# First stage of a four-layer convolution and attention network: the input norm moved a unit ahead on all engines, and the first query projection moved ahead of the value statistics

## The chip, the core and the metric

The kernel runs on one NeuronCore of a Trainium2 chip, as one program with one launch. The metric is the device time of one execution in microseconds (us). Lower is better. All arithmetic is float32.

## The reference, cut to what matters

The network has four residual layers on an image batch `x` of 8 images, 384 channels, 32x32 pixels. Only the head of layer 0 matters here:

```python
def _dwproj(x, dw, g, b, pw):                 # once each for q, k and v
    y = conv2d(x, dw, pad=1, groups=C)        # 3x3, one filter per channel
    y = gelu(batchnorm(y, g, b))              # mean and variance over all 8 images
    return einsum('oc,bchw->bohw', pw, y)     # 384 x 384 projection

h = groupnorm(x, 32 groups)                   # per image and group of 12 channels
q, k, v = _dwproj(h, ..q), _dwproj(h, ..k), _dwproj(h, ..v)
out = softmax(q^T k * hd**-0.5) v             # 8 heads of 48 channels, 1024 pixels
x = x + batchnorm(w_out @ out)
# layers 1 to 3: mixture of experts, depthwise + pointwise convolution,
# deformable attention; each on groupnorm(x), each added to x
```

The batch norm of q, k and v needs the statistics of the convolved images of the whole batch. So the convolutions of all eight images come first, their raw results go to DRAM, and only then can the first gelu, projection and attention start. That first part is called the first stage below.

## The kernel before, in words

**Units and items.** The stage works on 16 tiles `xs` of 128 partitions x 3072 numbers. Two tiles (`j` = 0, 1) make one *unit* `u`, and there are eight units. A unit is convolved in *items*, listed in `work` (lines 397 to 400): `y0 a1 y1 a2 v0` for units 0 to 5, `y0 a1 y1 a2` for unit 6, and `y0 a1 y1 a2 v-1 v0` for unit 7, which makes 40 items numbered `n`. Each item is a row of small matmuls on quarters and eighths of the array (line 554), into four PSUM banks: items of odd `n` take four single banks, items of even `n` two double ones. So the matmuls of an item can start when the item two before it has been copied out. ScalarE (ACT) copies the banks to a tile `y` (line 565; the pool of `y` has four buffers), VectorE (DVE) takes `bn_stats` of the four rows (line 571), and SyncE (SP) writes the tile to DRAM in four transfers (line 585).

**The norm.** Before a unit is convolved, its tiles are normalised in place. `norm(u)` (lines 326 to 394) gives five steps: `begin(0)` and `begin(1)` take statistics of the two tiles on DVE (lines 338, 341); `finish` is a chain of ten small DVE operations with one power on GpSimd (POOL) (lines 353 to 372), which ends in the scales `gss`; `apply(0)` and `apply(1)` each scale half of both tiles with two ACT instructions (line 384), after each of which POOL clears two border rows (line 387).

**Who sets the order.** The whole stage stands under a manual schedule: each engine executes its instructions in the order in which this loop issues them. In the item loop (from line 501) the steps of `norm(u + 1)` are issued during unit `u`, ahead of the item's matmuls, by the table

```python
        AT = {0: 0, 1: 1, 2: 2, 3: 3, 4: 3}
```

which says: `begin(0)` ahead of the unit's item 0, `begin(1)` ahead of item 1, `finish` ahead of item 2, and both `apply` steps, four ACT instructions in a row, ahead of item 3 (`a2`). Loads of later tiles and of the first raw images `g` are issued two per item on SP, in order with the `y` writes.

**The end of the stage.** Ahead of the last item but one, `spread_qk` (line 405) turns the statistics of q and k into scales: its scratch tile `room` is taken from the pool of `y`, so it waits until the write of an older `y` is done. After that item ACT applies gelu to the raw q image and the raw k image of image 0 (line 594), and DVE takes the moments of `x` (24 short `bn_aggr`, line 144). After the last item `spread_v` (line 459) does the same for v: statistics, a matmul `pmovev`, a chain on DVE, and the scales of v.

**The start of the attention.** Outside the manual schedule, only ACT keeps its issue order; the other engines' orders come from a scheduler. gelu of the v image, then `project(0, 0, v, h)` for q and k in two halves each (line 705), copied out in turn by ACT and DVE (`evac`), then `values` (line 678), scores (line 791), exponentials (line 798), and the weighted sum `pav` (line 806). The value tiles `vt` are zeroed by POOL (lines 653 and 660), with a dependency on the scales of v. Raw images live in the pool `im` of five buffers (`image`), taken in turn.

Of the kernel before, what the change touches and what calls it, by code (L numbers as in the profile page):

```python
# [7 lines left out]
F32 = mybir.dt.float32  # L8
# [5 lines left out]
N = H * W  # L14
P = 128
# [40 lines left out]
def tile_kernel(ctx: ExitStack, tc: tile.TileContext, i: dict, out: bass.AP):  # L56
# [196 lines left out]
    w0p = w0_ctx.enter_context(tc.tile_pool(name="w0", bufs=1))  # L253
    w_in = [w0p.tile([P, KC, C], F32, name=f"{nm}_sb") for nm in ("wq0", "wk0", "wv0")]

    with ExitStack() as pa:
        wa = pa.enter_context(tc.tile_pool(name="a_w", bufs=1))
        xa = pa.enter_context(tc.tile_pool(name="a_x", bufs=6))
# [63 lines left out]
        zv = wa.tile([P, 8, 2], F32, name="zv")  # L322
        fqk = wa.tile([P, 2, 2, KC], F32, name="fqk")
        fv = wa.tile([P, 2, KC], F32, name="fv")

        def norm(u):

            k, h = divmod(u, 2)
            mv = mvs[u % 2]
            turned = sa.tile([P, 2, 32], F32, tag="gp_t", name=f"gt{u}")  # L330
            rows = sa.tile([P, 2, 2, 16], F32, tag="gp_r", name=f"gr{u}")
            ss = sa.tile([P, 2, 32], F32, tag="gp_ss", name=f"gss{u}")
            small_ = sa.tile([P, 40], F32, tag="gp_s", name=f"gs{u}")

            def begin(j):
                for g in range(2):
                    for c in range(KC):
                        nc.vector.bn_stats(
                            xst[:, 2 * h + g, 2 * k + j, c, :], xs_of[2 * u + j][:, g * KC + c, :]
                        )  # L340
                    nc.vector.bn_aggr(
                        mv[:, :, 2 * j + g],
                        xst[:, 2 * h + g, 2 * k + j].rearrange("p c s -> p (c s)"),
                    )

            def finish():

                def owned(t):
                    return t.rearrange("p (g m d) -> p g m d", g=2, d=4)[:, :, :, 1:3]

                m8, v8, rs = small_[:, 0:2], small_[:, 2:4], small_[:, 4:6]
                dm, var, wide = small_[:, 8:40], turned[:, 1, :], [P, 2, 16]
# [19 lines left out]
                nc.vector.transpose(  # L372
                    ss.rearrange("p t y -> p (t y)"), rows.rearrange("p t g y -> p (t g y)")
                )

            def apply(g):
                for j in range(2):
                    n = 2 * j + g
                    d = xs_of[2 * u + j][:, g * KC : g * KC + KC, :]
                    sc, sh = ss[:, 0, n : n + 1], ss[:, 1, n : n + 1]  # L380
                    if u == 0 and j == 1:
                        nc.vector.tensor_scalar(d, d, sc, sh, ALU.mult, ALU.add)
                    else:
                        nc.scalar.activation(d, d, AF.Identity, bias=sh, scale=sc)
                    for e, row in enumerate((0, HALF - W)):
                        f = d[:, :, row : row + W]
                        nc.gpsimd.tensor_tensor(  # L387
                            f, f, mrow[:, e : e + 1].unsqueeze(2).to_broadcast([P, KC, W]),
                            ALU.mult,
                        )  # L390
# [12 lines left out]
        steps = {}  # L403

        def spread_qk():

            room = ya.tile([P, 4, HALF], F32, tag="y", name="room")
            zs, nv, ng = (zy, zqk.rearrange("p c g s -> p (c g) s")), (3, 2), 16
            both = [
                room[:, 0, 256 * t : 256 * t + 2 * n * ng].rearrange(  # L410
                    "p (v s g) -> p v s g", v=n, s=2
                ) for t, n in enumerate(nv)
            ]
            v0 = 0
            for z, n, dst in zip(zs, nv, both):
# [1 line left out]
                v0 += n  # L417
            yield
            pm = bank("pmove")
            for t, n in enumerate(nv):  # L420
                nc.tensor.matmul(
                    pm[:, 256 * t : 256 * t + 2 * n * ng], lhsT=sels[:, t, :],
                    rhs=room[:, 0, 256 * t : 256 * t + 2 * n * ng], start=True, stop=True,
                )
# [5 lines left out]
            fy = room[:, 3, :6].rearrange("p (v s) -> p v s", v=3)  # L430
            nc.vector.reduce_sum(fy.rearrange("p v s -> p (v s)"), got, AX.X)
            got = room[:, 2, :64].rearrange("p (x g) -> p x g", g=8)
            nc.vector.tensor_tensor(
                got, pm[:, 256:320].rearrange("p (x g) -> p x g", g=8),
                msk[:, 16:24].unsqueeze(1).to_broadcast([P, 8, 8]), ALU.mult,
            )
            f = room[:, 3, 8:16]
# [21 lines left out]
        def spread_v():  # L459

            both = sa.tile([P, 32], F32, tag="bothv", name="bothv")
            masked(zv, 2, 5, both.rearrange("p (c s g) -> p c s g", c=2, s=2))
            pm = bank("pmovev")
            nc.tensor.matmul(pm[:, :32], lhsT=sels[:, 1, :], rhs=both, start=True, stop=True)
            got = sa.tile([P, 4, 8], F32, tag="gotv", name="gotv")
# [30 lines left out]
        for f in norm(0):  # L496
            f()
        quads = [slice(32 * r, 32 * r + 32) for r in range(4)]
        loads = []
        LOADS = {0: (8, 9, 10), 1: (11, 12), 3: (13,), 4: (14, 15)}  # L500
        for n, (u, kind, s) in enumerate(work):
            k, h = divmod(u, 2)
            at = n - first[u]
            if at == 0:
# [99 lines left out]
    ost = const.tile([P, KC, 2 * B, 6], F32, name="ost")  # L604
# [35 lines left out]
    with ExitStack() as pb:  # L640
# [53 lines left out]
            load_image(fetched[b, t], o_dram[b] if t else x_img[b])  # L694

        def project(b, pr, v, h):
            if h == 0:
                qks[b, pr, v] = qp.tile([P, N], F32, tag=f"qk{v}", name=f"qk{v}_{b}_{pr}")
# [4 lines left out]
            pq = bank(f"pq{v}_{b}_{pr}_{h}")  # L703
            for c in range(KC):
                nc.tensor.matmul(  # L705
                    pq,
                    lhsT=w_in[v][:, c, pr * P : (pr + 1) * P],
                    rhs=rows_of(acts[b][v][:, c, :], h * H // 2, (h + 1) * H // 2) if v == 0
                    else acts[b][v][:, c, h * HALF : (h + 1) * HALF],
                    start=(c == 0),  # L710
                    stop=(c == KC - 1),
                )
# [1431 lines left out]
```

## Time and profile before

| | |
|---|---|
| median of 3 runs | 3521.9 us (3520.86 to 3522.46) |
| the profiled execution's own time | 3521.31 us |
| its span, first to last instruction | 3519.5 us, so 1.8 us lie around it |
| mean granted TensorE clock over the span | 0.981 |
| line 554, all matmuls of the stage | 3840 x, 175.7 us busy in sum, 66.1 us idle ahead of them |
| first matmul of the stage | 24.44 us |
| end of the stage's last item on TensorE | 243.42 + 1.25 = 244.67 us |
| first score matmul of image 0 | 267.03 us |
| first weighted sum `pav` of image 0 | 272.80 us |

The profile is one execution. A row of its timeline gives start, duration, engine, source line, operation, tiles, and in brackets how long the engine was idle before it and what ended that. PE is TensorE's matmuls, DVE VectorE, ACT ScalarE, POOL GpSimd, SP the queue that issues transfers. In the answer by stretches each row gives the busy time of each engine, then the granted TensorE clock, the mean busy share of the 16 DMA engines and the GB/s moved.

### The profile page before, as it was taken

Reading aid. Unit: us, or ns where it says so; the run is one execution under the profiler, and the core shown is the slowest. Engines: PE = TensorE matmul, PEld = TensorE weight load, DVE = VectorE, ACT = ScalarE, POOL = GpSimd, SP = SyncE. Lnnn points to the kernel's source line nnn. Section 1 sums busy time; section 2 is a strip of 40 time slices with the busy share of each in tenths; the row PEclk is TensorE's granted clock in tenths of the full one; section 3 lists DMA queues with packets and bytes.
Section 4 is the critical chain, followed back from the end, with each engine's and each line's share of the span. In section 5 each row is a group of like instructions: output and inputs, shape, how many; then the busy total and the mean of one; then the engine's idle time right before and its main releaser. Section 6 shows DMA issues by size and latency. Waiting matters only on the chain.

```text
span 3519.5 us, 44915 instructions
## 1 busy us (share of the span) xinstructions
PE 3379.2 (96%) x18599; PEld 1468.1 (42%) x18599; DVE 1695.2 (48%) x2881; ACT 1298.0 (37%) x1514; POOL 211.3 (6%) x231
## 2 busy tenths in 40 slices
PE   5879999999999999998999999999999999999897
PEld 2433434343434343433344444444443444534434
DVE  7762232323232323234266475564755647556663
ACT  4554444444444444433212323223233232332222
POOL 2110000000000000000000100101001010010112
PEclk9889999999999999999999999999999999999898
DMA  9872212112121212021700110101101011110000
GB/s 350 264 212 70 57 54 52 55 49 60 45 66 39 73 33 80 25 80 63 282 21 21 35 57 28 43 21 35 57 35 39 18 35 57 35 39 18 0 31 25
DMA packets 86259, 234.01 MB, mean 66 GB/s; under 512 B 21672, under 2 KB 21896, under 8 KB 79130
## 3 DMA queue, kind: packets, MB, share of 16 engines
q1 hardware_dynamic: 83882, 222.75, 20.0%
q10 hardware_dynamic: 1248, 4.72, 0.3%
q8 instruction: 150, 2.46, 0.3%
q0 software_dynamic: 912, 3.53, 0.3%
q14 instruction: 67, 0.55, 0.1%
HBM read 145.77 MB, written 75.59 MB: 63 GB/s over the span
## 4 chain that ended last, share of the span: by engine, by line
PE 41%; DVE 9%; DMA 1%; ACT 1%; POOL 0%; issue 0%; DVEq 0%; ACTq 0%; POOLq 0%; SPq 0%
PE y L1473 12%; PE ph L1452 9%; DVE y L1548 5%; PE pq L1593 4%; PE pw L1556 3%; PE pf L1900 3%; PE s L1771 2%; PE pav L1797 2%; DVE hd L1438 1%; DMA o<-o 1%; PE pk L1746 1%; PE pv L1755 1%; PE xsb L1732 1%; PE pss L1810 1%; PE plog L1202 1%; DVE off L1663 1%
## 5 line engine op out<-in xcount | busy, mean ns | idle before, releaser
L798 ACT ACTIVATE p<-s 128x1024 f32<-128x1024 f32 x512 | 496.4, 1021 | 365.9 <-PE s L791 365.5
L806 PE MATMUL pav<-p,vt 64*64 64x512 f32 x4096 | 494.5, 588 | 0.0
L1473 PE MATMUL y<-hd,w_sb 128*128 128x512 f32 x1080 | 488.5, 600 | 3.5 <-DVE hd L1438 3.5
L1452 PE MATMUL ph<-h,w_sb 128*128 128x512 f32 x1104 | 486.9, 595 | 4.7 <-ACT h L1401 4.7
L791 PE MATMUL s<-qk,qk 48*64 48x512 f32 x3072 | 370.5, 592 | 0.0
L1452 PEld LDWEIGHTS ph<-h,w_sb 128*128 128x128 f32 x1104 | 207.0, 190 | 266.1 <-issue 249.5
L1473 PEld LDWEIGHTS y<-hd,w_sb 128*128 128x128 f32 x1080 | 199.8, 191 | 248.1 <-issue 235.6
L806 PEld LDWEIGHTS pav<-p,vt 64*64 64x64 f32 x4096 | 167.4, 133 | 274.6 <-issue 274.4
L767 DVE COPY ta<-pav 128x512 f32<-128x512 f32 (+1 forms) x65 | 44.2, 682 | 475.5 <-PE pav L806 475.5
L554 PE MATMUL pk<-xs,cws_sb 32*32 32x496 f32 (+3 forms) x3840 | 175.7, 623 | 66.1 <-POOL xs L387 51.0
L1462 ACT ACTIVATE hd<-ph,b_sb 128x512 f32<-128x512 f32 x180 | 122.8, 682 | 312.3 <-PE ph L1452 312.3
L1548 DVE SCALAR_TENSOR_TENSOR y<-h,tap,y 128x961 f32<-128x961 f32 (+1 forms) x192 | 233.8, 1241 | 0.6
L1663 DVE SCALAR_TENSOR_TENSOR off<-q,dw_sb,off 128x225 f32<-128x225 f32 (+3 forms) x432 | 212.0, 546 | 1.6
L791 PEld LDWEIGHTS s<-qk,qk 48*64 48x64 f32 x3072 | 112.9, 133 | 221.1 <-issue 198.6
L81 DVE COPY qk<-pq 128x512 f32<-128x512 f32 x48 | 33.2, 691 | 260.5 <-PE pq L705 260.5
L1788 ACT ACTIVATE p<-s 128x1024 f32<-128x1024 f32 x96 | 96.1, 1023 | 166.5 <-PE s L1771 141.7
L554 PEld LDWEIGHTS pk<-xs,cws_sb 32*32 32x32 f32 (+1 forms) x3840 | 89.7, 116 | 150.4 <-issue 64.3
L1438 DVE TENSOR_TENSOR hd<-hd,cb 128x512 f32<-128x512 f32 x180 | 122.4, 685 | 40.9 <-ACT hd L1462 40.8
L1833 POOL TENSOR_TENSOR p<-p,p 128x1024 f32<-128x1024 f32 x48 | 113.0, 2356 | 349.3 <-ACT p L1788 349.3
L1556 PE MATMUL pw<-y,upw 128*128 128x512 f32 x288 | 129.6, 603 | 4.4 <-DVE y L1548 4.4
L705 PE MATMUL pq<-g,wq_sb 128*128 128x512 f32 x288 | 129.8, 601 | 0.0
L705 PE MATMUL pq<-g,wk_sb 128*128 128x512 f32 x288 | 129.2, 598 | 0.0
(318 smaller groups left out, 3692.5 us busy)
## 6 DMA issues: line engine op xcount, KB each, us to landing
rqk<-y SPq DMA_DIRECT2D x96, 256.0 KB
g<-rqk SPq DMA_DIRECT2D x96, 256.0 KB
xs<-in_xs_dram SPq DMA_DIRECT2D x56, 384.0 KB
g<-rv SPq DMA_DIRECT2D x48, 256.0 KB
xh<-in_x_dram SPq DMA_DIRECT2D x48, 256.0 KB
f<-in_x_dram SPq DMA_DIRECT2D x24, 512.0 KB
f<-o SPq DMA_DIRECT2D x24, 512.0 KB
o<-ot SPq DMA_DIRECT2D x42, 256.0 KB
```

The lines of the kernel that those rows point to most:

```text
L554: nc.tensor.matmul(banks[r][cols[q]].rearrange("p (h w) -> p h w", w=W)[:, :, c0:c1], lhsT=cws[rs, c, 2 * h + g, x, w], rhs=src[rs, :, c0 ...
L705: nc.tensor.matmul(pq, lhsT=w_in[v][:, c, pr * P : (pr + 1) * P], rhs=rows_of(acts[b][v][:, c, :], h * H // 2, (h + 1) * H // 2) if v == 0 ...
L791: nc.tensor.matmul(s[64 * k : 64 * k + 64, j * HALF : (j + 1) * HALF], lhsT=kt[r, k0 : k0 + 64], rhs=qt[r, h * HALF : (h + 1) * HALF], sta ...
L798: nc.scalar.activation(p, s, AF.Exp, scale=scale)
L806: nc.tensor.matmul(pav[k][64 * j : 64 * j + 64, :], lhsT=vts[b % 2][r, kc, 2 * hd : 2 * hd + 2, :].rearrange("p a b -> p (a b)"), rhs=p[r, ...
L1438: nc.vector.tensor_tensor(hd, hd, state["cb"], ALU.mult)
L1452: nc.tensor.matmul(ph, lhsT=w1[:, e, c, dc * P : (dc + 1) * P], rhs=state["h1"][c], start=(c == 0), stop=(c == KC - 1),)
L1473: nc.tensor.matmul(y, lhsT=w2[:, e, dc, m * P : (m + 1) * P], rhs=state[h, k], start=(k == 0), stop=(k == NE * KC - 1),)
L1548: nc.vector.scalar_tensor_tensor(d, f, tap2[:, c, t : t + 1], d, ALU.mult, ALU.add)
L1556: nc.tensor.matmul(pw[h], lhsT=upw2[:, c, m * P : (m + 1) * P], rhs=y[c][:, hs], start=(c == 0), stop=(c == KC - 1),)
L1593: nc.tensor.matmul(pq[h], lhsT=wq3[:, c, m * P : (m + 1) * P], rhs=h3[h][:, c, :], start=(c == 0), stop=(c == KC - 1),)
L1663: nc.vector.scalar_tensor_tensor(d, f, dw3[:, t : t + 1], d, ALU.mult, ALU.add)
```

## The change

Five edits, all in the first stage and at its end.

1. The steps of the norm have a new table. `apply` is cut into four steps, one ACT instruction with its two POOL instructions each, and these are issued ahead of items 1, 2, 3 and 4 of the unit before, one each. `begin(1)` and `finish` are issued ahead of item 0 of the unit before, and `begin(0)` ahead of the last item of the unit before that.
2. `room` is a tile of its own, not one from the pool of `y`.
3. Behind the last item but one only the q image gets its gelu; the gelu of the k image stands behind the last item's copies.
4. The projection of the first pair of heads of image 0 (`product`) stands at the end of the manual schedule: the q half ahead of the matmul of `spread_v`, the k half behind the scales of v. q is copied by ACT, k by DVE, into `first_qk`, which is a tile of the pool `im`.
5. The 24 moments of `x` come behind these copies on DVE.

```diff
-            def apply(g):
-                for j in range(2):
-                    n = 2 * j + g
...
+            def apply(g, j):
+                n = 2 * j + g
...
-            return [
-                lambda: begin(0), lambda: begin(1), finish, lambda: apply(0), lambda: apply(1)
+            return [lambda: begin(0), lambda: begin(1), finish] + [
+                lambda g=g, j=j: apply(g, j) for g in range(2) for j in range(2)
             ]
...
-        AT = {0: 0, 1: 1, 2: 2, 3: 3, 4: 3}
         first = [[w[0] for w in work].index(u) for u in range(NU0)]
         steps = {}
+        for u in range(1, NU0):
+            at = [(u - 2, 4) if u > 1 else (0, 0), (u - 1, 0), (u - 1, 0)]
+            at += [(u - 1, t) for t in range(1, 5)] if u < NU0 - 1 else [
+                (u - 1, 1), (u - 1, 2), (u - 1, 3), (u, 0)
+            ]
+            for t, key in enumerate(at):
+                steps.setdefault(key, []).append((u, t))
...
-            room = ya.tile([P, 4, HALF], F32, tag="y", name="room")
...
             both = sa.tile([P, 32], F32, tag="bothv", name="bothv")
             masked(zv, 2, 5, both.rearrange("p (c s g) -> p c s g", c=2, s=2))
+            yield
             pm = bank("pmovev")
...
-                steps = {}
-                for t, f in enumerate(norm(u + 1) if u + 1 < NU0 else ()):
-                    steps.setdefault(AT[t], []).append(f)
...
-            for f in steps.get(at, ()):
-                f()
+            for u1, t in steps.get((u, at), ()):
+                if t == 0:
+                    norms_of[u1] = norm(u1)
+                norms_of[u1][t]()
...
             if n == len(work) - 2:
                 gelu_image(acts[0][0], 0)
-                gelu_image(acts[0][1], 1)
-                for b in range(B):
-                    for m in range(KC):
-                        moments(xmv[:, b, m, :], xnst[:, b, m])
         assert not loads
-        spread_v()
-        scales = scale_of(2, fv)
+        gelu_image(acts[0][1], 1)
+        ends = spread_v()
+        next(ends)
+        first_qk = image("first_qk")
+        for v in range(2):
+            pq = big(f"pq{v}_first")
+            for h in range(2):
+                product(pq[:, h * HALF : (h + 1) * HALF], 0, 0, v, h)
+                (nc.vector.tensor_copy if v else nc.scalar.copy)(
+                    first_qk[:, v, h * HALF : (h + 1) * HALF], pq[:, h * HALF : (h + 1) * HALF]
+                )
+            if v == 0:
+                for _ in ends:
+                    pass
+                scales = scale_of(2, fv)
+        for b in range(B):
+            for m in range(KC):
+                moments(xmv[:, b, m, :], xnst[:, b, m])
...
         def project(b, pr, v, h):
+            made = b == 0 and pr == 0
...
-            evac(qks[b, pr, v][:, h * HALF : (h + 1) * HALF], pq)
+            if not made:
+                pq = bank(f"pq{v}_{b}_{pr}_{h}")
+                product(pq, b, pr, v, h)
+                evac(qks[b, pr, v][:, h * HALF : (h + 1) * HALF], pq)
```

`product` holds the three matmuls that stood in `project`. Otherwise the new `spread_qk` differs only in where it keeps its scratch (`room` and a small tile `fs`).

More of the change, by code (lines that the diff above doesn't have):

```diff
@@ L254, in tile_kernel, with product @@
     w_in = [w0p.tile([P, KC, C], F32, name=f"{nm}_sb") for nm in ("wq0", "wk0", "wv0")]
+    def product(pq, b, pr, v, h):
+        for c in range(KC):
+            nc.tensor.matmul(
+                pq,
+                lhsT=w_in[v][:, c, pr * P : (pr + 1) * P],
+                rhs=rows_of(acts[b][v][:, c, :], h * H // 2, (h + 1) * H // 2) if v == 0
+                else acts[b][v][:, c, h * HALF : (h + 1) * HALF],
+                start=(c == 0),
+                stop=(c == KC - 1),
+            )
     with ExitStack() as pa:
@@ L324, in tile_kernel @@
         fv = wa.tile([P, 2, KC], F32, name="fv")
+        room = wa.tile([P, 2, 160], F32, name="room")
+        fs = wa.tile([P, 16], F32, name="fs")
         def norm(u):
@@ L374, in finish @@
                 )
-            def apply(g):
-                for j in range(2):
-                    n = 2 * j + g
[L379 to L390, printed above, removed]
-            return [
-                lambda: begin(0), lambda: begin(1), finish, lambda: apply(0), lambda: apply(1)
+            def apply(g, j):
+                n = 2 * j + g
+                d = xs_of[2 * u + j][:, g * KC : g * KC + KC, :]
+                sc, sh = ss[:, 0, n : n + 1], ss[:, 1, n : n + 1]
+                if u == 0 and j == 1:
+                    nc.vector.tensor_scalar(d, d, sc, sh, ALU.mult, ALU.add)
+                else:
+                    nc.scalar.activation(d, d, AF.Identity, bias=sh, scale=sc)
+                for e, row in enumerate((0, HALF - W)):
+                    f = d[:, :, row : row + W]
+                    nc.gpsimd.tensor_tensor(
+                        f, f, mrow[:, e : e + 1].unsqueeze(2).to_broadcast([P, KC, W]),
+                        ALU.mult,
+                    )
+            return [lambda: begin(0), lambda: begin(1), finish] + [
+                lambda g=g, j=j: apply(g, j) for g in range(2) for j in range(2)
             ]
@@ L400, in tile_kernel @@
             work += [(u, w[0], int(w[1:])) for w in order.split()]
-        AT = {0: 0, 1: 1, 2: 2, 3: 3, 4: 3}
         first = [[w[0] for w in work].index(u) for u in range(NU0)]
         steps = {}
+        for u in range(1, NU0):
[5 more added lines that the diff above has]
+                steps.setdefault(key, []).append((u, t))
         def spread_qk():
-            room = ya.tile([P, 4, HALF], F32, tag="y", name="room")
             zs, nv, ng = (zy, zqk.rearrange("p c g s -> p (c g) s")), (3, 2), 16
+            at = [slice(0, 96), slice(96, 160)]
             both = [
-                room[:, 0, 256 * t : 256 * t + 2 * n * ng].rearrange(
-                    "p (v s g) -> p v s g", v=n, s=2
-                ) for t, n in enumerate(nv)
+                room[:, 0, d].rearrange("p (v s g) -> p v s g", v=n, s=2)
+                for d, n in zip(at, nv)
             ]
@@ L419, in spread_qk @@
             pm = bank("pmove")
-            for t, n in enumerate(nv):
+            for t, d in enumerate(at):
                 nc.tensor.matmul(
-                    pm[:, 256 * t : 256 * t + 2 * n * ng], lhsT=sels[:, t, :],
-                    rhs=room[:, 0, 256 * t : 256 * t + 2 * n * ng], start=True, stop=True,
+                    pm[:, d], lhsT=sels[:, t, :], rhs=room[:, 0, d], start=True, stop=True,
                 )
@@ L429, in spread_qk @@
             )
-            fy = room[:, 3, :6].rearrange("p (v s) -> p v s", v=3)
+            fy = fs[:, :6].rearrange("p (v s) -> p v s", v=3)
             nc.vector.reduce_sum(fy.rearrange("p v s -> p (v s)"), got, AX.X)
-            got = room[:, 2, :64].rearrange("p (x g) -> p x g", g=8)
+            got = room[:, 1, 96:].rearrange("p (x g) -> p x g", g=8)
             nc.vector.tensor_tensor(
-                got, pm[:, 256:320].rearrange("p (x g) -> p x g", g=8),
+                got, pm[:, 96:160].rearrange("p (x g) -> p x g", g=8),
                 msk[:, 16:24].unsqueeze(1).to_broadcast([P, 8, 8]), ALU.mult,
             )
-            f = room[:, 3, 8:16]
+            f = fs[:, 8:16]
             nc.vector.reduce_sum(f, got, AX.X)
@@ L498, in tile_kernel @@
         quads = [slice(32 * r, 32 * r + 32) for r in range(4)]
-        loads = []
+        loads, norms_of = [], {}
         LOADS = {0: (8, 9, 10), 1: (11, 12), 3: (13,), 4: (14, 15)}
@@ L594, in tile_kernel @@
                 gelu_image(acts[0][0], 0)
-                gelu_image(acts[0][1], 1)
-                for b in range(B):
-                    for m in range(KC):
-                        moments(xmv[:, b, m, :], xnst[:, b, m])
         assert not loads
-        spread_v()
-        scales = scale_of(2, fv)
+        gelu_image(acts[0][1], 1)
[8 more added lines that the diff above has]
+                    first_qk[:, v, h * HALF : (h + 1) * HALF], pq[:, h * HALF : (h + 1) * HALF]
+                )
+            if v == 0:
[5 more added lines that the diff above has]
+                moments(xmv[:, b, m, :], xnst[:, b, m])
     ost = const.tile([P, KC, 2 * B, 6], F32, name="ost")
@@ L696, in project @@
         def project(b, pr, v, h):
+            made = b == 0 and pr == 0
             if h == 0:
-                qks[b, pr, v] = qp.tile([P, N], F32, tag=f"qk{v}", name=f"qk{v}_{b}_{pr}")
+                qks[b, pr, v] = first_qk[:, v, :] if made else qp.tile(
+                    [P, N], F32, tag=f"qk{v}", name=f"qk{v}_{b}_{pr}"
+                )
                 if pr == 0:
@@ L702, in project @@
                     )
[L703 to L712, printed above, removed]
-            evac(qks[b, pr, v][:, h * HALF : (h + 1) * HALF], pq)
+            if not made:
+                pq = bank(f"pq{v}_{b}_{pr}_{h}")
+                product(pq, b, pr, v, h)
+                evac(qks[b, pr, v][:, h * HALF : (h + 1) * HALF], pq)
             if h == 1:
```

## The prediction

> **What bounds the kernel now.** I read the page, then the answer by stretches, then the timeline of one unit, then that of the stage's end. The page says that TensorE carries the whole:
>
> ```profile
> span 3519.5 us, 44915 instructions
> PE 3379.2 (96%) x18599; PEld 1468.1 (42%) x18599; DVE 1695.2 (48%) x2881; ACT 1298.0 (37%) x1514; POOL 211.3 (6%) x231
> PE   5879999999999999998999999999999999999897
> ```
>
> Only the first three slices (88 us each) are below 9, and the stage ends near 267 us. From there PE is full (33.00 of 33.00 us in 267 to 300), so what the stage gives reaches the end unreduced. By stretches, two units and a restart inside one:
>
> ```profile
> 81.72:109.19 27.47, 22.59 (x486) 11.67 (x478) 21.66 (x47) 16.00 (x18) 3.31 (x9) 0.87 0.93 288
> 109.19:137.09 27.90, 22.77 (x494) 11.87 (x485) 21.66 (x47) 16.12 (x20) 3.30 (x9) 0.87 0.76 233
> 104.50:110.20 5.70, 5.70 (x45) 3.93 (x48) 5.70 (x10) 3.18 (x5) 0.16 (x1) 0.52 0.90 280
> ```
>
> A unit lasts 27.5 to 27.9 us (mean 27.74 over the five from 53.81 to 192.53), and no engine fills it: PE 22.6, DVE 21.7. So a loop of waits sets it. The timeline shows it:
>
> ```profile
> 97.31 0.24 DVE L372 STREAM_TRANSPOSE gss<-gr 128x64 f32<-128x64 f32 x1
> 97.47 2.43 DVE L571 BATCH_NORM_STATS2 sy<-y 128x6 f32<-128x512 f32 x4
> 97.59 6.34 ACT L384 ACTIVATE xs<-xs,gss 128x1536 f32<-128x1536 f32 x4 [6.47 <-DVE gss L372]
> 103.83 3.84 ACT L565 COPY y<-pk 128x512 f32<-128x512 f32 x6
> 104.43 2.47 DVE L571 BATCH_NORM_STATS2 sqk<-y 128x6 f32<-128x512 f32 x4 [4.53 <-ACT y L565]
> 106.82 2.46 DVE L571 BATCH_NORM_STATS2 sv<-y 128x6 f32<-128x512 f32 x4
> 109.19 1.27 DVE L338 BATCH_NORM_STATS2 xst<-xs 128x6 f32<-128x512 f32 x2
> ```
>
> DVE reaches `gss` 15.8 us after the unit's start at 81.72 (two begins of 4.05, two item statistics of 2.35, finish 3.0). ACT, idle for it, does four applies, and only then copies a2 and v0, for whose statistics DVE waits 4.53. 15.8 + 6.3 + 0.5 + 4.8 = 27.4: the loop is closed. PE idles 4.8 us in it, and restarts at half clock (0.52 in the third row by stretches). The stage's end:
>
> ```profile
> 252.12 0.61 PE L464 MATMUL pmovev<-bothv,sels_sb 128*128 128x32 f32 x2 [7.45 <-DVE bothv L454]
> 252.54 7.47 PE L705 MATMUL pq<-g,wq_sb 128*128 128x512 f32 x12
> 255.53 3.50 ACT L243 ACTIVATE g<-g,ss 128x1024 f32<-128x1024 f32 x3 [5.76 <-DVE ss L485]
> 255.69 6.96 POOL L653 MEMSET vt<- 128x4096 f32 x2 [0.78 <-DMA gbo_sb<-in_gbo_dram]
> 262.60 0.54 POOL L660 MEMSET vt<- 128x128 f32 x2
> 272.80 1.90 PE L806 MATMUL pav<-p,vt 64*64 64x512 f32 x16
> ```
>
> PE waits 7.45 us for the statistics of v and only then projects q, which had been ready; the zeroing of `vt` ends at 263.1, 9.7 before `pav`.
>
> **The change, part by part.** *Nothing is saved in work.* The moved norm steps are 12 statistics and 14 small DVE operations, one power (0.70) and eight border rows (0.35 each) on POOL, four applies on ACT per unit; no transfer moves with them. POOL's power still stands ahead of its unit's border rows. What changes is who stands behind whom.
>
> *Unit 0.* `begin(1)` and `finish` now follow `begin(0)` at once: 23.80 + 4.05 + 4.05 + 3.0 = 34.9 (before, 42.2). y0's statistics queue behind them and wait about 4 us; the four `y` buffers cover that. ACT: apply 1.6, a1 copies 2.05, to 38.55. a2 needs a1's banks: 3.3 on PE, 0.85 for a half clock that may follow the 3 us gap, v0 7.0, tail to the end of its statistics 3.2, `begin(1)` and `finish` 7.05: the scales of unit 2 at 60.0, against 69.65.
>
> *Units 1 to 5.* The new loop: `gss` releases apply 1.6, then a1's copies 2.05 (now behind one apply), which free the banks for a2; a2; v0 7.0 (its own banks come free sooner); copies and statistics 3.2; and behind these on DVE `begin(1)` 4.05 and `finish` 3.0. **The new wait** is ACT's for `finish`, directly behind y0's copies: a1's and y1's copies queue behind it, and PE stands still once y1 is convolved. a2 at full clock takes 3.3, and this loop 24.2; but then DVE's own order is longer: `gss`, ACT's three applies and a1, y1, a2 copies 10.9, last statistics 0.7, `begin(0)` 4.05, v0 2.4, 7.05, sum 25.1. PE's burst (v0, y0, a1, y1 and a2) is 7.0 + 2.85 + 3.3 + 2.85 + 3.3 = 19.3, so its gap is near 5 us. *What the row says:* after gaps of 4.8, 4.1 and 5.8 us (ahead of 104.5, 132.4 and 187.9) the trace's clock is 0.52, 0.52 and 0.56 over the next 5.7, 5.1 and 4.5 us. *The rule against this change:* the Trainium skill, "TensorE: Matmul & The Clock Gate" (Part 1: The HAM clock gate), says that an idle window of about 3.4 us throttles and about 3.4 us of busy time releases; so a shorter loop that keeps such a gap keeps the penalty. By the row, about 5 us at half clock lose 2.5, a2 takes 5.75, and the loop is 26.65; by the rule's 3.4 us it would lose 1.7 and be 25.9. I take 26.7, by the row: five loops give 60.0 + 133.5 = 193.5 for the scales of unit 7, against 209.33: 15.8 gained.
>
> *Unit 7.* From there apply, a1 copies, a2 (5.75) 9.4; a1 of unit 7 waits for the fourth apply and its border rows until 13.75; a1, y1, a2, v 16.4; the matmul of `spread_qk` 0.7 (its 3.9 us wait for a `y` write is gone, hidden now behind v's 7.0); v 7.0: 37.9, so the last item ends at 231.4. Before it took 35.3, since the applies had been ahead. E = 244.67 becomes 231.4: 13.3 gained.
>
> *The end, counted from E.* q's first half 2.6 at once, but both halves lie in one double bank, and the second half waits for ACT's copy of the first. ACT has y39's copies 2.0 and now k's gelu 3.5 ahead of that copy: second half 6.1 to 8.7, `pmovev` 9.2, DVE chain 2.75, scales of v 12.05. (Before: 10.8, counted from its E.) k's first half and its copy, a third of `values` behind gelu of v, k's second half to 16.25, copy 17.0, scores 17.0. Before: 22.4. So far 5.4 gained. **But** `vt` lies where first-stage tiles lay, those that the moments read (`xnst`) among them, so its zeroing now waits for the last of the moments on DVE, no longer for the scales, and the moments stand behind k's copies: 17.0 + 1.8 + 0.2 + 6.96 + 0.3 = 26.3. `pav` cannot start sooner; with gelu of q perhaps ending 1 us behind E, 26.8 against 28.1 before. The gap of 4 us ahead of it costs a half clock again, 2.5 by the row. So the end gives back 1.2.
>
> *Transfers.* SP's order of writes and loads is kept; only the loads of image 1 move, since `first_qk` takes a buffer of `im`: the k image's six wait for the last `values` (about 294), the q image's six for the k projection of pair 2 (about 348.5); their gelus come at 344 and 382, so 40 and 27 us cover this. Uncovered, each us late would stall ACT's gelu and the exponentials queued behind it. Less time per unit does ask more of DMA. Stores alone run at 232 and 256 GB/s (133.5 to 140 and 106 to 112.4, DMA share 0.93 and 0.90), loads at 431 (20 to 30). A unit stores 4.72 MB, 19.3 us, and loads 1.57 MB per tile, 3.65 us: 28.5, 24.8, 23.0, 26.6 for units 1 to 4, mean 25.7, just under 26.7. A second rule speaks against the change: the skill's "SBUF — State Buffer" (Door 1: The DMA port swizzle) gives a transfer on 32 partitions 8 of 16 ports, about 218 GB/s, and a `y` store has 32 or 16. By it the mean is 28.0, more than a unit takes now, and the loop gains nothing. The measured stores beat it, so I take the row, but for unit 1, the fullest, charge 2 us.
>
> *Sum.* 13.3 - 1.2 - 2 = 10. Own time 3519.5 + 1.8 = 3521.3, less 10 is 3511.3; the median stands 0.6 above that execution: 3512.
>
> **The rivals.** *Longer gain:* the burst reaches PE's gap so that the clock does not drop, and units take DVE's 25.1: 1.6 x 5 = 8 more, 18 in all, 3504. For it: DVE and ACT alone allow it. Against: the gap is then longer still, 5.8 us. *Transfers hold the units:* share 0.93 is little room, and unit 1 is now at 314 GB/s. Units 1 to 5 then stay near 27.7, of the 15.8 some 10 remain from unit 0's head start, less 2.6 in unit 7, 1.2 and the last units' burst of writes 2: gain 4, 3518. *Slower:* PE's burst is broken by short waits for banks, so that no busy window releases the clock. At half clock throughout, 19.3 us of a unit become 38.6. One further window of 3.4 us costs 1.7; the gain of 10 is used up by six windows in all, and from ten on, three for every two units, it is over 0.2% slower, 3530. Against: v0, y0, a1 and y1 are fed ahead and last 16 us. *The change fails to do what it says* for the value sums: q does start before `pmovev`, but its second half does not; that is in the sum.
>
> **How the numbers follow.** 0.2% is 7.0 us, about what a measurement can tell from no change. The main case 0.62, 3507 to 3516, of which an eighth is within 0.2%; longer gain 0.15; transfers 0.18, nearly all within 0.2%; slower 0.05. So faster 0.70, same 0.25, slower 0.05. The range 3503 to 3518 leaves out the far end of the longer gain and the worst of the last two.
>
> **What would show it right or wrong.** In the profile after: units of 26.7 on DVE, four single applies per unit; ACT idle ahead of the first of them; a PE gap near 5 us after y1 with 0.5 clock behind it; PE's last item ending near 231 to 235; a projection of q split by a wait for ACT; `vt` zeroed only behind the moments, `pav` waiting for POOL. Wrong, if units are 25 or 27.7, if SP lags so that copies of `y` wait for writes, or if `pav` follows the exponentials directly.

## The result and the profile after

The changed kernel takes 3508.25 us (median of 6 runs, 3505.04 to 3510.91) against 3522.18 us for the kernel before on the same chip (6 runs, 3520.86 to 3526.64): ratio 0.9958, 95% interval 0.9946 to 0.9971, 13.9 us saved where 10 were forecast. The profiled execution of the changed kernel is its shortest, 3505.04 us for a span of 3503.2.

The page after. TensorE has the same work; its first three slices read 6, 8 and 8 tenths where they read 5, 8 and 7:

```profile
PE 3380.1 (96%) x18599; PEld 1467.3 (42%) x18599; DVE 1697.7 (48%) x2881; ACT 1297.4 (37%) x1514; POOL 211.0 (6%) x231
PE   6889999999999999998999999999999999999888
L570 PE MATMUL pk<-xs,cws_sb 32*32 32x496 f32 (+3 forms) x3840 | 175.4, 643 | 52.7 <-ACT y L581 26.0
```

The last row is the group of the conv items: half of the idle time ahead of them (26.0 of 52.7) is now the wait for ScalarE's copies ahead of a2 (seven waits).

By stretches (us, busy us of each engine with instruction counts, granted TensorE clock, DMA share, GB/s), two units from one `gss` to the next, and the stage's end:

```profile
61.36:87.30 25.94, 21.97 (x480) 11.26 (x480) 22.02 (x47) 16.02 (x18) 3.30 (x9) 0.87 0.91 305
87.30:113.30 26.00, 21.93 (x480) 10.95 (x480) 22.06 (x46) 16.02 (x20) 3.30 (x9) 0.93 0.91 295
228.58:267.00 38.42, 30.72 (x137) 12.83 (x138) 10.67 (x55) 17.38 (x20) 8.27 (x5) 1.00 0.56 154
```

A unit lasts 26.0 us. A clock of 0.87 over 25.94 us is 6.7 us at half clock, 0.93 over 26.00 is 3.6; behind 228.58 the clock stays at 1.00. The timeline of the second of these units:

```profile
87.30 0.25 DVE L385 STREAM_TRANSPOSE gss<-gr 128x64 f32<-128x64 f32 x1
87.58 1.67 ACT L396 ACTIVATE xs<-xs,gss 128x1536 f32<-128x1536 f32 x1 [5.32 <-DVE gss L385]
89.15 2.02 ACT L581 COPY y<-pk 128x512 f32<-128x512 f32 x4
89.77 21.99 PE L570 MATMUL pk<-xs,cws_sb 32*32 32x512 f32 x480 [3.53 <-ACT y L581]
95.98 2.08 ACT L581 COPY y<-pk 128x512 f32<-128x512 f32 x4
99.02 1.86 DVE L351 BATCH_NORM_STATS2 xst<-xs 128x6 f32<-128x512 f32 x3
103.89 2.47 DVE L587 BATCH_NORM_STATS2 sv<-y 128x6 f32<-128x512 f32 x4 [0.74 <-ACT y L581]
106.28 1.86 DVE L351 BATCH_NORM_STATS2 xst<-xs 128x6 f32<-128x512 f32 x3
```

The wait that was forecast is there: ScalarE waits for `gss`, does one apply, and copies a1; TensorE, which had stood still for 3.53 us, starts a2 0.6 us into those copies. What closes the unit is VectorE's order behind that: a2's copies end at 98.06 and their statistics a microsecond later, `begin(0)` starts at 99.02, the statistics of v0 follow at 103.89, `begin(1)` starts at 106.28 (the last line), and `finish` brings the next `gss` at 113.30. VectorE waits for v0's copies 0.74 us here, about 0.5 us in another of the five units and not at all in three. The end of the stage, in order of time:

```profile
208.63 7.50 SPq L508 DMA_DIRECT2D xnst<-xst  x8
...
218.26 1.07 SPq L601 DMA_DIRECT2D rv<-y  x2
222.24 1.93 ACT L581 COPY y<-pk 128x1024 f32<-128x1024 f32 x2 [6.34 <-DVE ss L496]
...
234.19 0.58 ACT L620 COPY first_qk<-pq_first 128x512 f32<-128x512 f32 x1
234.82 2.84 PE L258 MATMUL pq_first<-g,wq_sb 128*128 128x512 f32 x6 [3.47 <-ACT first_qk L620]
...
248.09 6.96 POOL L681 MEMSET vt<- 128x4096 f32 x2 [8.10 <-DVE xmv L144]
255.36 1.95 PE L830 MATMUL pav<-p,vt 64*64 64x512 f32 x16 [2.79 <-POOL vt L688]
```

q is projected from 228.51, but its second half starts at 234.82, behind the copy at 234.19, and in between ScalarE makes y39's copies and the gelu of k; `pmovev` runs at 237.50 and the scores at 246.62; `vt` is zeroed from 248.09, behind the moments; `pav` waits for that. The first `pav` starts at 255.36 instead of 272.80: 17.4 us gained where the stage ends. Of these, 8.0 us are there at the scales of unit 2 already (61.61 against 69.65), the five units up to the scales of unit 7 add 9.8, unit 7 gives back 1.7 (37.1 us from its scales to its last item against 35.3), and the end gains 1.3 (26.8 us against 28.1). Behind that point the two kernels do the same work, and there the changed one took 1.1 us longer (3247.9 us to the end of its span against 3246.7). Over the fourteen profiled kernels this remainder lies between 3246.7 and 3250.9. So an effect inside the stage is read below from the start of the first `pav`, and the median is told beside it.

### The profile page after: what moved, and what is told of

The parts are those of the page before. It is cut to its first block, busy times and chain, and to the rows that moved or that the text cites. A ratio compares the mean times of both kernels' runs of the same rounds, so it can differ in the third digit from the quotient of the medians.

```text
span 3503.2 us, 44910 instructions
## 1 busy us (share of the span) xinstructions
PE 3380.1 (96%) x18599; PEld 1467.3 (42%) x18599; DVE 1697.7 (48%) x2881; ACT 1297.4 (37%) x1514; POOL 211.0 (6%) x231
## 3 DMA queue, kind: packets, MB, share of 16 engines
q0 software_dynamic: 912, 3.53, 0.3%
## 4 chain that ended last, share of the span: by engine, by line
PE 42%; DVE 9%; ACT 1%; DMA 1%; issue 0%; POOL 0%; DVEq 0%; ACTq 0%; SPq 0%; POOLq 0%
PE y L1497 12%; PE ph L1476 9%; DVE y L1572 5%; PE pq L1617 4%; PE pw L1580 3%; PE pf L1924 3%; PE s L1795 2%; PE pav L1821 2%; DVE hd L1462 1%; PE pk L1770 1%; PE pv L1779 1%; PE pss L1834 1%; DMA o<-o 1%; PE xsb L1756 1%; PE plog L1226 1%; DVE off L1687 1%
## 5 line engine op out<-in xcount | busy, mean ns | idle before, releaser
L815 PE MATMUL s<-qk,qk 48*64 48x512 f32 x2944 | 355.1, 592 | 0.0
L570 PE MATMUL pk<-xs,cws_sb 32*32 32x496 f32 (+3 forms) x3840 | 175.4, 643 | 52.7 <-ACT y L581 26.0
L815 PEld LDWEIGHTS s<-qk,qk 48*64 48x64 f32 x2944 | 109.3, 133 | 211.4 <-issue 190.5
L706 PE MATMUL pv<-wv_sb,g 128*128 128x384 f32 x384 | 127.2, 489 | 1.4 <-ACT g L243 1.4
L815 PE MATMUL s<-ql,ql 48*64 48x512 f32 x1024 | 128.2, 592 | 0.2 <-ACT p L822 0.2
```

Of the source, the lines that this page charges most:

```text
L570: nc.tensor.matmul(banks[r][cols[q]].rearrange("p (h w) -> p h w", w=W)[:, :, c0:c1], lhsT=cws[rs, c, 2 * h + g, x, w], rhs=src[rs, :, c0 ...
L706: nc.tensor.matmul(pv[:, :C], lhsT=acts[b][2][:, c, t * P : (t + 1) * P], rhs=w_in[2][:, c, :], start=(c == 0), stop=(c == KC - 1),)
L815: nc.tensor.matmul(s[64 * k : 64 * k + 64, j * HALF : (j + 1) * HALF], lhsT=kt[r, k0 : k0 + 64], rhs=qt[r, h * HALF : (h + 1) * HALF], sta ...
```

## The experiments

All times in us. "Saved" is the median of the kernel before in the same comparison less the kernel's own; the ratio has its 95% interval. "Scales 7" is the end of `gss` for unit 7, E the end of the last conv item on TensorE, y38 the start of ScalarE's copy of the item ahead of that one (the last but one, v of the unit before).

| kernel | scales 7 | E | y38 | first pav | median | saved | ratio |
|---|---|---|---|---|---|---|---|
| before | 209.3 | 244.7 | 237.7 | 272.8 | | | |
| changed | 191.5 | 228.6 | 222.2 | 255.4 | 3508.3 | 13.9 | 0.9958 (0.9946-0.9971) |
| norm_alone | 191.6 | 232.8 | 225.4 | 260.9 | 3511.4 | 12.7 | 0.9965 (0.9951-0.9979) |
| end_alone | 210.1 | 242.1 | 234.7 | 270.1 | 3520.6 | 3.5 | 0.9993 (0.9984-1.0001) |
| y1_twice | 189.7 | 226.4 | 220.6 | 255.2 | 3507.4 | 16.6 | 0.9951 (0.9938-0.9965) |
| begins_early | 175.7 | 222.5 | 219.3 | 255.2 | 3505.7 | 15.8 | 0.9949 (0.9936-0.9963) |
| applies_together | 183.1 | 221.1 | 216.5 | 251.3 | 3504.6 | 16.9 | 0.9952 (0.9939-0.9966) |
| end_mended | 191.4 | 228.9 | 223.4 | 252.5 | 3502.0 | 22.0 | 0.9940 (0.9926-0.9954) |
| moments_early | 190.5 | 227.2 | 223.3 | 255.1 | 3504.1 | 17.4 | 0.9950 (0.9936-0.9964) |
| q_copy_first | 191.4 | 228.0 | 222.4 | 252.2 | 3502.8 | 21.3 | 0.9943 (0.9930-0.9957) |
| end_split | 192.4 | 229.3 | 222.9 | 248.6 | 3496.7 | 24.8 | 0.9929 (0.9915-0.9942) |
| rows_alone | 193.5 | 231.3 | 222.2 | 259.5 | 3508.7 | 15.4 | 0.9959 (0.9946-0.9973) |
| both | 184.8 | 222.0 | 218.2 | 243.9 | 3494.4 | 29.7 | 0.9915 (0.9902-0.9929) |
| both_rows | 182.3 | 220.3 | 215.6 | 241.3 | 3491.9 | 32.3 | 0.9913 (0.9898-0.9928) |

**The change taken apart: norm_alone and end_alone.** Each is the kernel before with one part of the change: the table of norm steps with single applies, or everything from `spread_qk` on.

> Only the norm steps are changed; the end of the stage is that of the kernel before. Theory (the loop of norm waits carries the gain): units of 26.0 us as in the changed kernel, the last conv item ends 12 to 16 us earlier than before (the 3.9 us wait of the q and k sums for a y buffer may come back), the end takes about 28 us from there: 3507 to 3511 us. Rival (the two parts share the gain, the end being worth half): 3514 to 3516 us. Rival (transfers hold the units once they are asked for sooner): 3518 us.

> Only the end is changed (q projected ahead of the value sums, moments last, own memory for the sums); the norm steps are those before. Theory: units stay at 27.7 us; the value weights' first product starts about 27 us after the last conv item instead of 28.1, and the 3.9 us wait for a y buffer may fall away: a gain of 1 to 5 us, 3517 to 3521 us. Rival (half of the gain is the end's): 3515 us. As the prediction costed it (gives back 1.2, with a half clock of 2.5 us): about 3521 us.

norm_alone's first `pav` is 11.9 us earlier than before, end_alone's 2.7: the norm steps carry most of it, and in both the theory held, for norm_alone at the edge of its range (for end_alone the interval of the ratio includes 1, so there only the trace shows a gain). In the timeline of norm_alone's TensorE, what the end change takes away is still there, a wait ahead of `pmove` and 7.00 us ahead of `pmovev`:

```profile
222.98 0.91 PE L426 MATMUL pmove<-room,sels_sb 128*128 128x96 f32 x4 [3.04 <-issue]
239.77 0.60 PE L469 MATMUL pmovev<-bothv,sels_sb 128*128 128x32 f32 x2 [7.00 <-DVE bothv L459]
```

The two parts make 14.6 us at `pav`, the whole change 17.4. Part of the missing 2.8 lies in the clock. end_alone has the same split of q as the changed kernel, and its second half runs half slow. Its timeline:

```profile
248.11 4.31 PE L258 MATMUL pq_first<-g,wq_sb 128*128 128x512 f32 x6 [3.23 <-ACT first_qk L616]
```

The six products take 4.31 us here (the clock is 0.88 over 242.11 to 256.00) and 2.84 in the changed kernel, behind a gap of 3.23 us here and 3.47 there.

**What the half clock costs: y1_twice.** The products of y1 are made a second time in the gap ahead of a2, in the same banks, with nothing else moved.

```diff
-            for p in passes:
+            again = kind == "y" and s == 1 and u < NU0 - 1
+            for p in passes + passes * again:
```

> The changed kernel, but the products of each unit's y1 item are made twice over in the same banks (units 0 to 6), so that TensorE works 2.85 us into the gap of 3.4 to 4.4 us ahead of a2, with nothing else moved. Theory (the half clock behind the gap costs 1.7 to 3.4 us per unit on the loop, and VectorE's own order takes 25.4): no half clock behind these gaps, units of 25.4 instead of 26.0, and unit 7 some 2 us shorter: 3502 to 3505 us. Rival (the clock does not count, the loop is VectorE's and ScalarE's): 3508 us. Rival (the added products push a2 and v0 back): units of 27 or more, 3514 us or more.

One of its units by stretches, and then the second half of q in its timeline:

```profile
61.60:87.10 25.50, 23.81 (x560) 10.49 (x544) 21.96 (x47) 15.91 (x18) 3.31 (x9) 1.00 0.92 313
```

```profile
233.22 4.24 PE L258 MATMUL pq_first<-g,wq_sb 128*128 128x512 f32 x6 [4.01 <-ACT first_qk L621]
```

More work on TensorE did not make the units longer: the clock stays at 1.00 in five of the six, and a unit lasts 25.6 us on the mean of five instead of 26.0. But the seven kernels that have the changed kernel's unit steps without the added products lie between 25.8 and 26.4, so 0.4 us per unit is hardly more than their scatter, and the median is where the rival had it that gives the clock no part. Those seven kernels show the same without any added work. Of their 35 units, the two with no half clock last 25.8 us on the mean, the seventeen with one piece of it (3.4 us) 26.0, and the sixteen with 6.8 us 26.1. The unit of moments_early that starts at 86.92 is the second unit shown above, at full clock (its stretch, then VectorE's `begin(1)`):

```profile
86.92:112.92 26.00, 22.46 (x498) 9.28 (x485) 22.07 (x46) 16.02 (x20) 3.30 (x9) 1.00 0.94 300
105.90 1.86 DVE L351 BATCH_NORM_STATS2 xst<-xs 128x6 f32<-128x512 f32 x3
```

In both, `begin(1)` comes 18.98 and the next `gss` 26.00 us behind `gss`, with 3.6 us at half clock in the one and none in the other. So the half clock hardly reaches the loop that sets a unit.

In y1_twice E came 2.2 us earlier, and only 0.2 of it is left at `pav`, 255.2: y38 was copied 1.6 us earlier, the wait for q's copy grew to 4.01 us, and this time half clock followed it (4.24 against 2.84).

**Which half of the norm edit matters: applies_together and begins_early.** The first puts the four applies back in one row ahead of a2's copies and leaves `begin` and `finish` a unit ahead. The second takes `begin(1)`, too, out of the way of `finish`.

```diff
 applies_together
-            at += [(u - 1, t) for t in range(1, 5)] if u < NU0 - 1 else [
-                (u - 1, 1), (u - 1, 2), (u - 1, 3), (u, 0)
-            ]
+            at += [(u - 1, 3)] * 4
 begins_early
-            at = [(u - 2, 4) if u > 1 else (0, 0), (u - 1, 0), (u - 1, 0)]
+            at = [(u - 2, 1), (u - 2, 4)] if u > 1 else [(0, 0), (0, 0)]
+            at += [(u - 1, 0)]
```

> The changed kernel, but the four applies of a unit stand together ahead of a2's copies, as in the kernel before; statistics and finish stay a unit ahead. Theory (what counts is that finish lies ahead; ScalarE then does a1's and y1's copies without waiting for it): units no longer than 26.0, perhaps VectorE's 24 to 24.5: 3500 to 3508 us. Rival (the single applies carry the gain, since 6.4 us of applies in a row hold back the copies of a2 and v0): units of 27 us or more, 3515 us or more.

> The changed kernel with begin(0) of a unit at a1 and begin(1) at v0 of the unit two before, so that only finish stands between the statistics of v0 and the scales. Theory (the loop of waits sets the unit, and with 4.15 us taken out of it VectorE's own 23.8 us do): units of 24 to 24.5 us instead of 26.0, the last conv item 7 to 10 us earlier, 3500 us. Rival (transfers hold the units at the 25.7 us worked out of the store and load rows): units of 25.7, 1 to 2 us gained, 3507 us. Rival (begins now wait for image tiles that have not landed): no gain or slower.

In both the loop is broken. Units last 24.6 us (applies_together) and 23.4 us (begins_early), on the mean of the five up to unit 7's scales. The single applies carry nothing: with the four in one row ScalarE no longer has to wait for `finish` ahead of a1's copies, because by the time it reaches the applies `finish` is done. Its waits for `gss` from 35 us on (us in total, times, longest), in the changed kernel up to 229 and in applies_together up to 186:

```profile
ACT xs L396 <- DVE gss L385: 39.6, 7, 6.7
```

```profile
ACT xs L396 <- DVE gss L385: 1.8, 1, 1.8
```

Now other waits appear, the longest of this kind in applies_together from 35 to 186, and one of begins_early from 190 to 247:

```profile
ACT y L579 <- DMA rqk<-y: 27.1, 9, 4.1
```

```profile
ACT y L582 <- DMA rv<-y: 8.4, 1, 8.4
```

ScalarE's copies wait for `y` buffers whose stores have not landed; no such row stands among the changed kernel's waits up to 229. How much of this the units of applies_together pay is not shown; the 8.4 us are begins_early's y38. begins_early's median of 3505.7 is thus near that of its rival on transfers, though its units are those of the theory. SP's queue shows the same from its side, changed kernel first, then applies_together:

```profile
SPq L601 <- ACT y L581: 17.9, 16, 2.9
```

```profile
SPq L599 <- ACT y L579: 4.8, 8, 1.1
```

The changed kernel's queue still waits 17.9 us in all for copies to store; with shorter units most of that slack is used up, and begins_early gives back in unit 7 what it gained: its scales of unit 7 come 15.8 us earlier than the changed kernel's, its last conv item 6.1, its `pav` 0.2.

**The end: end_mended, moments_early, q_copy_first, end_split.** moments_early moves the 24 moments directly behind `next(ends)`; q_copy_first does the copy of q's first half ahead of the gelu of k; end_mended does both; end_split adds separate banks for the four halves.

```diff
 moments_early
         next(ends)
+        for b in range(B):
+            for m in range(KC):
+                moments(xmv[:, b, m, :], xnst[:, b, m])
 q_copy_first
-        gelu_image(acts[0][1], 1)
...
+                if v == 0 and h == 0:
+                    gelu_image(acts[0][1], 1)
 end_split
-            pq = big(f"pq{v}_first")
             for h in range(2):
-                product(pq[:, h * HALF : (h + 1) * HALF], 0, 0, v, h)
+                pq = bank(f"pq{v}_{h}_first") if v else big(f"pq{v}_{h}_first")[:, :HALF]
+                product(pq, 0, 0, v, h)
```

> The changed kernel with two moves at the end: the 24 moments directly behind the value sums' products on VectorE, so that the zeroing of vt waits only for the scales; and ACT's copy of the first half of q ahead of the gelu of k. Theory (the chain q copy, second half, pmovev, scales of v is 3.4 us late for the gelu, and vt is 2.8 us late for the moments): pav starts near 249 us instead of 255.4, 3502 us. Rival (the exponentials with their table load hold pav anyway): pav near 252, 3505 us. Rival (neither wait counts): 3508 us.

> The changed kernel with the 24 moments moved alone (directly behind the value sums' products on VectorE). Theory (of the two moves of end_mended the moments carry all of it, since the scores came no earlier there): vt zeroed from 241, pav straight behind the exponentials near 252.4 instead of 255.4, about 3 us under the changed kernel: 3505 us. Rival (each move carries half): pav near 254, 3506.5 us.

> The changed kernel with ScalarE's copy of q's first half ahead of the gelu of k, moments left last. Theory (ScalarE's chain is 3.5 us shorter to the copy, but the second half of k stands behind the gelu of v and its own copy, and the zeroing of vt still waits for the moments behind that): pmovev 2 to 3.5 us earlier, pav within 0.7 us of the changed kernel's, 3508 us. Rival (the copy carries its own part of the gain of end_mended): pav 2 to 3 us earlier, 3505.5 us.

> end_mended, and the halves of the first q and k products in separate banks instead of one double bank, so that no second half waits for the copy of the first. Theory (the waits for these copies hold the scores): q's second half right behind the first, scales of v near E+8.7 instead of E+12, scores near E+14 instead of E+18, no half clock at 240, pav near E+19 instead of E+23.7: about 5 us under end_mended, 3497 us. Rival (gelu of v, table load and exponentials hold pav anyway): pav within 1.5 us of end_mended's, 3501 us.

end_mended's `pav`, 252.5, came where the rival had it (252), not at 249. The moments do what was said: in moments_early `pav` follows its scores by 5.77 us (8.74 in the changed kernel), without a wait for POOL:

```profile
255.10 1.90 PE L830 MATMUL pav<-p,vt 64*64 64x512 f32 x16
```

But the scores came 2.7 us later, since y38 was copied 1.0 us later and q's second half met half clock (4.54 us), so the first `pav` gained only 0.3, where 3 had been expected. The expectation for q_copy_first was wrong: with the moments still last, `pav` came 3.2 us earlier. Everything behind q's copy moved up with it, the gelu of v, k's second half and the moments, and the wait of 2.8 us for POOL stayed the same size at an earlier time (half clock follows it here: 3.46 us for 16 products):

```profile
244.90 6.96 POOL L682 MEMSET vt<- 128x4096 f32 x2 [8.11 <-DVE xmv L144]
252.17 3.46 PE L831 MATMUL pav<-p,vt 64*64 64x512 f32 x16 [2.79 <-POOL vt L689]
```

I had taken the copy to be worth nothing because in end_mended the scores still stood at 246.69. Two accidents of that execution hid its worth: y38 was copied 1.2 us later than in the changed kernel, and half clock fell on k's second half (3.86 us instead of 2.74; the clock is 0.95 over the 31 us behind E). end_split has none of these waits:

```profile
229.19 5.42 PE L258 MATMUL pq_first<-g,wq_sb 128*128 128x512 f32 x12
```

Both halves of q are one run of 12 products, the scores come 13.6 us behind E instead of 18.0, `pav` 19.3 instead of 26.8, as expected.

**What starts the end: rows_alone.** In the changed kernel ScalarE's chain behind y38 has no gap: copy, table load, gelu of q, copies of y39, gelu of k, copy of q. Counted from y38's copy, `pav` comes 33.1 us later in the changed kernel, 29.8 in q_copy_first, and 25.7 in each of end_split, both and both_rows. But y38 is the start only where it is late: in ten of the twelve kernels with the new end, y39's copies start 6.65 us behind y38's, and in end_alone and rows_alone, where E comes later than that, at E. In the changed kernel the two lie 0.3 us apart. And y38 takes the buffer of y34, whose stores stand on SP's queue behind eight transfers of statistics (`xnst`, 7.50 us). rows_alone keeps whole rows of 576 bytes together in `xnst` instead of pieces of 24.

```diff
-        xnst = wa.tile([P, B, KC, 2, 6], F32, name="xnst")
+        xnst = wa.tile([P, 2, B, KC, 6], F32, name="xnst")
```

> The changed kernel with one layout changed: the statistics of x are moved between partitions in whole rows (576 bytes) instead of pieces of 24 bytes, so that these eight transfers no longer take 7.5 us of SP's queue at 208.6 to 216.1. Theory (the copy of y38 at 222.24 waits for y34's stores, queued behind these transfers, not for the VectorE row that the trace names): y38 is copied as soon as TensorE is done with it, near 220.2, the gelu of q starts 1.4 us earlier, y39's copies 0.7 to 1.4 earlier, and pav by as much: 3507 us; units before 205 stay at 26.0, since no copy waits for a transfer there. Rival (transfers hold the stage): the units and the end come 5 us or more earlier, 3503 us. Rival (the row named is the true cause): nothing moves, 3508 us.

The transfers took 6.58 us, not the small part of 7.50 that was hoped for, so y38 was copied at 222.21, as in the changed kernel, and the test does not decide. The later `pav`, 259.5, is not the edit's doing as far as the trace shows: the scales of unit 7 were already 2.0 us later, which is inside the spread of the seven kernels with the same unit steps (190.5 to 193.5), and q's second half met half clock (4.51). In favour of the buffer as the cause: this time the trace names it.

```profile
217.57 1.57 SPq L601 DMA_DIRECT2D rv<-y  x2
222.21 1.93 ACT L581 COPY y<-pk 128x1024 f32<-128x1024 f32 x2 [4.55 <-DMA rv<-y]
```

So it does in six of the twelve kernels that have their own memory for the sums, and in all twelve y38's copy follows the end of those stores on the queue by 2.4 to 4.0 us. An edit that moves the stores alone was not tried, so this stays a reading of the traces.

**A version that beats both: both, both_rows.** both is end_split with the applies together; both_rows adds the row layout.

> end_split with the four applies together as in applies_together. Theory (the gains add): last conv item near 221, pav 19.4 us behind it near 241, about 7 us under end_split: 3490 us. Rival (transfers, which stood behind 15 copies of y in applies_together, hold the end): pav near 244.6, 3493 us. Rival (no gain over end_split): 3497 us.

> both, with the statistics of x moved in whole rows as in rows_alone. Theory (with units of 24.6 us the transfers are what holds unit 7: its copies of y waited 2.1 and 4.45 us for stores): the last conv item 3 to 6 us earlier than in both, pav near 237: 3486 us. Rival (VectorE's sums hold the end): within 1 us of both, 3490 us.

ScalarE's copy of y38 in both:

```profile
218.20 1.93 ACT L579 COPY y<-pk 128x1024 f32<-128x1024 f32 x2 [6.61 <-DMA rv<-y]
```

both reached 243.9, not 241: `pav` follows y38's copy by the same 25.7 us as in end_split, and y38 was copied only 4.7 us earlier although E came 7.2 earlier, as its rival said. both_rows is 2.65 us better at `pav` (241.3, not the 237 expected); its scales of unit 7 were 2.5 us earlier too, so the row layout is not shown to be the reason, and the medians, 3491.87 (3490.42 to 3497.28) and 3494.44 (3492.30 to 3495.07), do not part them. Either saves twice what the change did.

## Why the prediction was right, and where it only came out right

Most of its mechanism is what the trace shows: the same work, ScalarE's wait for `gss`, the gap ahead of a2 with half clock behind it, the split of q, `vt` behind the moments, `pav` behind `vt`. The loop that sets a unit is not the one that it chose. Step by step:

- *Units 1 to 5, taken at 26.7.* Measured 26.0, and by another loop. The prediction took the loop through a2 and v0, 24.2 at full clock, and made it 26.65 by a half clock behind the gap. The half clock came and hardly counted (the unit of moments_early; 0.4 us between y1_twice and this kernel). What closes a unit is VectorE's own order, which the prediction had summed to 25.1 and left to a rival. Its terms, mean of five units with the prediction's in brackets: from `gss` to the end of a2's copies 10.7 (10.9), the last statistics 1.3 (0.7), `begin(0)` 4.1 (4.05), a wait for v0's copies 0.2 (none), v0's statistics 2.35 (2.4), `begin(1)` and `finish` 7.3 (7.05). That a loop that does not bind, with a penalty that hardly counts, came out 0.7 us from the one that does is luck. Five loops: 3.6 us more gained than forecast.
- *a1's copies, 2.05.* This term was too long: from `gss` to a2 it was 2.5 us (mean of five), not 3.65, since a2 starts 0.6 us into the copies, not behind the last.
- *The clock in these units.* The rule of the Trainium skill ("TensorE: Matmul & The Clock Gate", Part 1: The HAM clock gate), as the prediction read it, would have had some 3.4 us at half clock per unit. The stretches give 6.7 or 3.6 us at half clock per unit, 5.4 on the mean of the five, so the row's 5 was the better size. That the unit came out at the rule's 25.9 all the same is chance: the unit does not follow either length.
- *Unit 0, scales of unit 2 at 60.0.* Measured 61.6: `gss` ended at 35.3 instead of 34.9, and from there VectorE's order took 26.35 us, of which 1.08 are a wait for v0's copies that stood in no sum. Half clock was not the reason: norm_alone and q_copy_first, with a clock of 1.00 from 35 to 61.3, reach these scales at 61.4 and 61.5. 1.6 less gained.
- *Unit 7, 37.9.* Measured 37.1: 0.8 more.
- *The end.* Second half of q at E + 6.2 (6.1), `pmovev` at E + 8.9 (9.2), scores at E + 18.0 (17.0), `pav` at E + 26.8 (26.8). The "2.5" for a half clock behind the wait for `vt` did not come: 1.00. That was this execution's luck: behind the same wait of 2.79 us q_copy_first and begins_early took 3.46 and 3.60 us for the 16 products instead of 1.95, and end_alone, y1_twice, moments_early and rows_alone each paid 1.4 to 1.7 us on q's second half. The anchor was only half right: the chain starts at E or 6.65 us behind y38's copy, whichever is later, and in the changed kernel the two fall together. In applies_together, both and begins_early E comes 2.1 to 3.5 us earlier than the other.
- *Transfers, 2.* They cost nothing in the units; begins_early ran at 23.4 us, below the mean of 25.7 that had been worked out from store and load rows, so that estimate was no floor, and still less the 28.0 estimated from the 218 GB/s of the Trainium skill's "SBUF — State Buffer" (Door 1: The DMA port swizzle), which the stores measured in the kernel before, 232 and 256 GB/s, had already beaten. Where transfers seem to count is unit 7, through the buffer of y38.

In all: -1.6 + 3.6 + 0.8 + 2.5 + 2 = 7.3 on top of 10, and 17.4 measured at `pav`. So within the stage, in the profiled execution, which is the fastest of the six, the step sums were too low by 7. That is the size of the rival *longer gain*, and half its mechanism: VectorE's order does set the units, at 26.0 and not 25.1, but the clock did drop. The median came near the forecast because the rest went the other way: 1.1 us behind the stage in the profiled execution, and a median 3.2 above that execution where 0.6 was allowed. That too is luck.

*Slower* was excluded by the units at 26.0, and its mechanism failed where it could have shown: in applies_together TensorE's work is broken by fourteen short waits (0.3 to 1.6 us) and the clock is 1.00 in all six units. These short waits brought no half clock; in the changed kernel one wait of 3 to 5 us per unit did. *Transfers hold the units* did not come about here; it may be the next bound: the traces of six kernels name a store as what y38's copy waits for, for 8.4 us in begins_early.

## What to carry to other kernels

When a norm step is moved ahead, look for the engine that issues its consumers in order: in the changed kernel ScalarE still waits between 4 and 7 us per unit for `finish`, because the first of four single applies makes it ask early; with the four in one row it asks later, and the units are 1.4 us shorter. Where two loops come out close, sum both with every wait in them: here the one left aside was the one that held. Charge a copy that frees banks one at a time with its first bank only. A gain inside a stage is kept only if the end of the stage is fed by the same chain; find what starts that chain (here, as far as the traces tell, a buffer whose store stood behind eight small transfers) before counting a microsecond, and give two halves that are projected in turn their own banks.

## What the runs showed of the hardware that I had not expected

- Whether half clock follows a wait of TensorE varies from one execution to the next. Waits of 3.23 (end_alone, rows_alone), 4.01 and 4.66 us were followed by it, the changed kernel's 3.47 us by none. The wait of 2.79 us ahead of `pav` was followed by it in q_copy_first and begins_early, and not in the changed kernel. The waits ahead of a2 (3.4 to 4.4 us) brought 3.6 us of half clock in one unit and 6.7 in the next. 1 to 2 us of the end hang on it; in the units no loss was seen beyond the 0.4 us of y1_twice.
- Eight transfers of 18 KB each took 7.50 us on SP's queue in pieces of 24 bytes, and 6.58 us in rows of 576 bytes with 24 times fewer packets: 0.9 and 0.8 us each. So the size of the pieces made little difference; the number of transfers was not varied.
- 2.85 us of useless products per unit did not make the stage longer: E came 0.7 us earlier than in the earliest of the seven kernels with the same unit steps, and the first `pav` 0.2 us earlier than the changed kernel's.
